# A fused four-layer network: 3x3 convolution in quarters with a fixed TensorE order, neighbour rankings in three steps, and quarter-size convolutions from contiguous copies

## The chip, the cores and the metric

One core of one Trainium2 chip runs the whole program as a single launch. The metric is the device time of that launch in microseconds. In a core, TensorE (PE in the profile; its weight loads are PEld) multiplies matrices from SBUF into PSUM, VectorE (DVE), ScalarE (ACT) and GpSimd (POOL) work on tiles in SBUF and PSUM, and DMA queues move data between the device's memory and SBUF; here nearly all bulk transfers are issued by SyncE (SP), and some by ScalarE. Each engine runs its own instructions in order and waits on semaphores for the others. Everything is float32.

## The reference, cut to what matters

`x` has shape (8, 64, 128, 128): eight images of 64 channels. Four layers follow each other, each with a residual and a group normalisation in front:

```python
x = x + deformable_conv(_gn(x), ...)    # layer 0
x = x + conv3x3(_gn(x), weight)         # layer 1: 64 -> 64 channels, padding 1
x = x + two_S5_blocks(_gn(x), ...)      # layer 2: one scan along rows, one along columns
x = x + neighbours(_gn(x), ...)         # layer 3
```

Layer 3, in short:

```python
x1 = relu(bnorm(conv2d(x, wd, bd, 4, 0)))          # 4x4 kernel, stride 4: 32x32 pixels remain
d2 = sq[:, :, None] + sq[:, None, :] - 2 * einsum("blc,bmc->blm", xt, xt)   # pixel to pixel
...                                                # window of 7x7 pixels, 9 largest distances
out = mean(x_final - xt[:, :, None, :], axis=2)    # mean of the nine picked, minus own
cat = concatenate([x1, out_img], axis=1)
feat = relu(bnorm(conv2d(cat, w1, b1, 1, 1)))      # 3x3, 128 -> 64 channels
att = sigmoid(bnorm(conv2d(mean(feat), wa)))       # one factor per image and channel
return resize(feat * att, 128x128, "bilinear")     # enlarged by 4
```

## The kernel before, in words

**Tiling.** Two images of 64 channels fill the 128 partitions, so there are four *pairs* of images. One pair is 128 x 16384 floats, and SBUF holds two such *rooms*. Layer 0 is done first for all pairs (most of its time is an indirect DMA that gathers pixels, L380, and VectorE's weighted sums of them, L391 and L392). It ends near 11700 us. Then `rest` (L496) takes the pairs p = 0 to 3 in turn: `conv3x3` (layer 1), `scan_layer` (layer 2), and `neighbours` (layer 3). The room that a pair doesn't fill holds that pair's normalised copy during the convolution; during the scans it is free, or receives the next pair.

**`neighbours` is a generator.** The one of pair p is not run when it is made; `conv3x3` of pair p + 1 is handed it as `aside`, and takes a step of it with `next(aside, None)` between its own operations. So three of the four convolutions (p = 1, 2, 3) have the previous pair's layer 3 beside them. Layer 3 of the last pair runs alone at the very end.

**`conv3x3` (L603 to L659).** Each of 16 loads normalises eight rows (L626, ScalarE) and SP's DMAs distribute them into `two`: row pairs on the free axis, and the odd and even rows of a pair on the two halves of the partitions, so that one product contracts 2 rows x 64 channels. The loop over n (16 steps) computes eight rows per image: for each parity e of the output row, each of two row pairs m, each of three column shifts dx and each image i there is a product (L647) of 128 x 64 weights with 4 rows of 128 pixels into the PSUM tile `c`, and the last is followed by an addition into the image (L651, VectorE). Where m is not e, half of the weights are zeros. For p = 0 these products are cut to *quarters*: only the half of the partitions whose weights are not zero, and products for e = 0 and e = 1 alternate, so that with the two images they use all four quarters of TensorE's array. For p = 1 to 3 the products are full: I call six products over all partitions a *block*; the quarters of a step, twelve products of a quarter of the array each, count as one too. A full step has four blocks, a step in quarters three (e = 0, the quarters, e = 1). Each float32 product has two records in the trace, so a full step has 48. There are three `next(aside)` per step. The program doesn't set the order between these products and those of `aside`; the Tile scheduler does, for every engine.

**`neighbours` (L1066 to L1181)** has three parts.

1. The quarter-size convolution, `quarter` (L983 to L1033) where a convolution is beside it: eight times, 16 rows of the stored image are loaded by four DMAs that ScalarE issues (L1007, three buffers), and 16 products (L1031) of 128 x 64 weights with 128 pixels read every fourth column of them, straight from the loaded rows; ScalarE's Relu (L1032) writes `x1`. For the last pair the image is still in SBUF, and `quarter_here` (L1035) reads it there: 16 taps x 2 images x 2 halves of the image, each product (L1055) with 512 pixels at a column step of four.
2. The ranking. For both images and each of eight pieces of 128 pixels, `farthest` (L1201) multiplies the piece with up to 320 pixels around it (L1207, the distance `d`), ScalarE adds the pixel's own square (L1211, `d2`), and VectorE does the rest: window (L1214, `key`), largest eight, replaced, the ninth, replaced, and a 0/1 `mask` (L1224). `means` (L1226) turns the mask with TensorE (L1232, `st`), ScalarE copies it (L1234, `sel`), and three products (L1238, `po`) with `xt` average the picked pixels into the second half of `cat` (L1239). `means` of a piece is called after `farthest` of the next. `features` (L1185) is the 3x3 convolution over `cat`, in four sets of 18 products (L1197, `pf`), and comes as soon as the pieces that it needs are done. Before the loop, `xt` (L1115) and the squares `own` (L1119) are made by TensorE, ScalarE and VectorE.
3. The enlarging. After the mean (L1137), the attention (L1142) and the scaled feature map (L1148, `wide`), each strip of eight small rows is widened (L1162 ScalarE, L1163 VectorE, into `up`), and for each of eight pieces of the image and each of four row phases VectorE adds two weighted rows of `up` onto the image (L1178, L1179: 64 operations of 128 x 512 in all), and SP stores the piece to `out` (L1180).

**The scans.** `scan_layer` runs class `Turns`: 16 groups of eight rows forward, then 16 more (`G >= NG`), all engines in an order written out by a planner. `at` (L1620) gives every operation a time, from the table `BESIDE` for the first half and `ALONE` for the second, plus a multiple of the group's planned length (26.969 and 27.485 us); the operations are sorted by that time and emitted under `manual_schedule()`. In the trace a group of the last scan's second half takes 13.19 us. Of one group, the operations used below are: `uv` (L1651, an addition on POOL), `xsb` and `xs` (L1662 and L1663, subtractions on POOL), `pn` (L1319) and the output products `py` (L1361) on TensorE, the turned copies `pt` (L1268, ScalarE), and the addition of a finished half group into the image, `add0` and `add1` (L1422, VectorE). For pairs 0 to 2 (`follow` is set) each finished group is also stored, `kept`, and the next pair is loaded beside; for the last pair neither happens.

Other rows that serve as prices: L1284 (ScalarE's normalisation in the scans, which reads every fourth element), L1282 and L1106 (POOL, a wide step and 1024 elements), L1531 (POOL, a copy of repeated elements).

Of the kernel before, what the change touches and what calls it, by code (L numbers as in the profile page):

```python
# [9 lines left out]
F32 = mybir.dt.float32  # L10
I32 = mybir.dt.int32
AF = mybir.ActivationFunctionType
ALU = mybir.AluOpType
# [3 lines left out]
P = 128  # L17
# [25 lines left out]
class Net:  # L43
# [452 lines left out]
    def rest(self):  # L496
        tc, nc = self.tc, self.nc
        with ExitStack() as ctx:
# [14 lines left out]
            for p in range(self.npair):  # L513
                now, other = rooms[p % 2], rooms[(p + 1) % 2]
                a, b = image(now), image(other)
                r, nb = self.conv3x3(p, a, other, *self.gn1, aside)
                norm = self.scan_layer(p, a, b, r, nb)
                aside = self.neighbours(p, None if p + 1 < self.npair else now[:, 0:HW], norm)
# [82 lines left out]

    def conv3x3(self, p, a, room, r, nb, aside):
# [8 lines left out]
        with self.tc.tile_pool(name=f"b_conv{p}", bufs=1) as cp, self.tc.tile_pool(name=f"b_conv2_{p}", bufs=2) as wp:  # L611
# [18 lines left out]
            for n in range(0, H // 2, 4):  # L630
                quarters = p == 0
                sets = []
                for e in range(2):
                    full = [(e, m, slice(0, P)) for m in range(2) if m == e or not quarters]
                    sets += [[(e, m, rows, dx) for dx in (0, -1, 1) for _, m, rows in full]]
                if quarters:
                    sets.insert(1, [(e, 1 - e, half[e], dx) for dx in (0, -1, 1) for e in range(2)])
                po = [None, None]
                left = [6, 6]
                for e, m, rows, dx in chain(*sets):  # L640
                    if po[e] is None:
                        po[e] = self.ps.tile([P, 4, H], F32, tag="b", name=f"c1_{p}_{n}_{e}")
                    c0, c1 = max(0, -dx), min(H, H - dx)
                    left[e] -= 1
                    for i in range(2):
                        mv = two[rows, i, n + m : n + m + 4, c0 + dx : c1 + dx]
                        nc.tensor.matmul(po[e][half[i], :, c0:c1], lhsT=w[rows, e, m, dx + 1], rhs=mv, start=left[e] == 5, stop=left[e] == 0)  # L647
                    if left[e]:
                        continue
                    rows = a[:, 2 * n : 2 * n + 8, :].rearrange("p (m e) w -> p e m w", e=2)[:, e]  # L650
                    nc.vector.tensor_add(rows, rows, po[e])  # L651
                    next(aside, None)
                for k in range(2):
                    g = n // 2 + k
                    nc.vector.bn_stats(st[:, g, :], a[:, 4 * g : 4 * g + 4, :].rearrange("p h w -> p (h w)"))
                next(aside, None)
            for _ in aside:
                pass
# [325 lines left out]
    def quarter(self, sp, p, src, norm, x1):  # L984
# [4 lines left out]
        with self.tc.tile_pool(name=f"b_down{p}", bufs=1) as wp, self.tc.tile_pool(name=f"b_down2_{p}", bufs=3) as yp:  # L989
# [13 lines left out]
            def load(n):  # L1003
# [4 lines left out]
                loaded.append(y.rearrange("p i (h m) (w g) -> p i h m w g", m=2, g=4))  # L1008
# [15 lines left out]
            for n in range(8):  # L1024
                if n + 2 < 8:
                    load(n + 2)
                yv = loaded.pop(0)
                pd = self.ps.tile([P, 4, S], F32, tag="x", name=f"pd{p}_{n}")
                for t in range(8):
                    for i in range(2):  # L1030
                        nc.tensor.matmul(pd[half[i]], lhsT=wr[i][:, t, :], rhs=yv[:, i, :, t // 4, :, t % 4], start=t == 0, stop=t == 7)  # L1031
                nc.scalar.activation(x1[:, n * P : (n + 1) * P], pd.rearrange("p h w -> p (h w)"), AF.Relu, bias=off, scale=self.bnd[0])  # L1032
                yield  # L1033

    def quarter_here(self, sp, p, af, norm, x1):  # L1035
# [4 lines left out]
        with self.tc.tile_pool(name=f"b_down{p}", bufs=1) as wp:  # L1040
# [8 lines left out]
            view = af.rearrange("p (h u f w g) -> p h f g u w", h=2, f=4, w=S, g=4)  # L1049
            pd = [self.ps.tile([P, L // 2], F32, tag="b", name=f"pd{p}_{i}") for i in range(2)]  # L1050
            for t in range(16):
                for i in range(2):
                    for h in range(2):
                        to = pd[i][half[h]].rearrange("p (u w) -> p u w", w=S)
# [11 lines left out]
    def neighbours(self, p, here, norm):  # L1066
# [3 lines left out]
        with tc.tile_pool(name=f"b_near{p}", bufs=1) as sp:  # L1070
# [10 lines left out]
            else:  # L1081
                yield from self.quarter_here(sp, p, here, norm, x1f)
            place = (lambda i, m: (m, i)) if here is None else (lambda i, m: (4 * i + m % 4, m // 4))
            with tc.tile_pool(name=f"b_far{p}", bufs=2) as wp:
# [8 lines left out]

                def filled(t, to, k):
# [17 lines left out]
                for m in range(2):  # L1112
                    tp = self.ps.tile([P, 4, P], F32, tag="y", name=f"xt{p}_{m}")
                    for k in range(4):
                        nc.tensor.transpose(tp[:, k, :], x1f[:, (4 * m + k) * P : (4 * m + k + 1) * P], self.ident)  # L1115
                    nc.vector.tensor_copy(xt[:, 4 * m : 4 * m + 4, :], tp)
                    sq = wp.tile([P, 8, C], F32, tag="sq", name=f"sq{p}_{m}", bufs=1)
                    nc.scalar.activation(sq.rearrange("p a c -> p (a c)"), tp.rearrange("p k c -> p (k c)"), AF.Square)
                    nc.vector.tensor_reduce(own[:, 4 * m : 4 * m + 4].rearrange("p k i -> p (k i)"), sq, axis=mybir.AxisListType.X, op=ALU.add)  # L1119
# [3 lines left out]
                late = None  # L1123
                for t in range(L // P):
                    for i in range(2):
                        mask = masks[0] if t == 0 else masks[3] if t == L // P - 1 else masks[1 + i]
                        self.farthest(wp, i, t, cat, xs, own, place, mask, f"{p}_{i}_{t}")
                        if late:
                            self.means(wp, *late)
                        late = i, t, mask, cat, xt, place, f"{p}_{i}_{t}"  # L1130
                        yield
                        if i == 0 and t in (3, 5, 7):
                            self.features(p, t // 2 - 1, cat, w1, feat, total, "x" if here is None else "b")
                self.means(wp, *late)
                self.features(p, 3, cat, w1, feat, total, "x" if here is None else "b")
# [7 lines left out]
            with tc.tile_pool(name=f"b_up{p}", bufs=2) as wp:  # L1143
# [8 lines left out]
                R = self.STRIP  # L1152
                for n in range(8):
                    if n % (R // 4) == 0:
                        h0 = 4 * n
                        up = wp.tile([P, R + 2, H], F32, tag="up", name=f"up{p}_{n}")
                        uv = up.rearrange("p h (w g) -> p h w g", g=4)
                        r0, r1 = max(0, h0 - 1), min(S, h0 + R + 1)
                        m0, m1 = r0 - h0 + 1, r1 - h0 + 1
                        for k, (side, w_side, w_mid) in enumerate(phases):  # L1160
                            t = wp.tile([P, R + 2, S], F32, tag="t", name=f"up_t{p}_{n}_{k}")
                            nc.scalar.mul(t[:, m0:m1], wide[:, r0:r1, 1 + side : S + 1 + side], w_side)  # L1162
                            nc.vector.scalar_tensor_tensor(uv[:, m0:m1, :, k], wide[:, r0:r1, 1 : S + 1], w_mid, t[:, m0:m1], ALU.mult, ALU.add)  # L1163
                        if h0 == 0:
                            nc.vector.tensor_copy(up[:, 0, :], up[:, 1, :])  # L1165
                        if h0 + R == S:
# [620 lines left out]
```

## Time and profile before

| | |
|---|---|
| runs | 15335.88, 15339.65, 15353.08 us; median 15339.65 |
| profiled execution | 15356.15 us, of which the span in the trace is 15354.2 |
| mean granted clock of TensorE | 0.821 |
| busy, share of the span | PE 66%, PEld 24%, DVE 75%, ACT 21%, POOL 68% |
| instructions | PE 32812, DVE 27082, ACT 5480, POOL 10624 |
| layer 0 and what it sets up | until some 11700 us |
| first convolution, first to last product | 11763.9 to 11893.6 us (130) |
| the three convolutions with layer 3 beside them | from 12523, 13419 and 14319 us: 271, 273, 271 |
| the last scan's second half | 14980 to 15195 us |
| the last pair's layer 3 | 15205 us to the end |

A row of a windows view has a stretch in us from the span's start, its length, and each engine's busy time in it with the number of instructions; then the clock that TensorE was granted (1.00 is full), the share of the DMA engines and the bytes moved. A row of a groups view has the line, the engine, the operation, what it writes <- what it reads with shapes, the number; after the bar the busy us, the mean ns of one, and the idle time before them with what ended it. A timeline row has the start, the duration, and the same names; brackets give a wait in us and who ended it.

### The profile page before, as it was taken

What the parts mean: (1) busy time and instruction counts of PE and PEld (TensorE: products, weight loads), DVE (VectorE), ACT (ScalarE), POOL (GpSimd) and SP (SyncE); (2) the same over time, 40 slices, a digit from 0 to 9 for tenths busy, and PEclk for the clock granted to TensorE, in tenths of its full rate; (3) what the DMA queues carried; (4) which work ended last, traced back from release to release, by engine and by line L of the source; (5) the groups of instructions that cost most, each with busy time, mean ns of one, the idle gap of its engine ahead of it and who ended that gap; (6) DMA issues with size and microseconds to landing.
All of it is one profiled execution on the core that took longest, in us unless ns stands there. A gap on an engine that the chain in (4) does not pass through costs nothing. (4 is left out here: it accounts for less than half of the span.)

```text
span 15354.2 us, 121942 instructions
## 1 busy us (share of the span) xinstructions
PE 10117.0 (66%) x32812; PEld 3654.0 (24%) x32812; DVE 11461.6 (75%) x27082; ACT 3228.7 (21%) x5480; POOL 10386.9 (68%) x10624
## 2 busy tenths in 40 slices
PE   7774477537765563577556656655434888899887
PEld 2211122112211111122111111111111444444443
DVE  6777777777777777777777777777775867858687
ACT  1100011001100000111000000000001855638374
POOL 5777777777777777777777777777773643617163
PEclk9986698759877786798777888887656999999998
DMA  5444454435543333444333333333333453544441
GB/s 175 125 123 132 122 152 154 125 116 153 154 130 113 115 116 111 138 150 127 114 114 115 116 115 115 118 117 110 108 108 121 107 138 115 141 113 125 130 105 54
DMA packets 888915, 1893.98 MB, mean 123 GB/s; under 512 B 198044, under 2 KB 447012, under 8 KB 866212
## 3 DMA queue, kind: packets, MB, share of 16 engines
q0 software_dynamic: 442368, 1208.55, 26.9%
q1 hardware_dynamic: 388192, 648.04, 14.0%
q10 hardware_dynamic: 57668, 29.59, 0.9%
q8 instruction: 265, 4.34, 0.1%
q14 instruction: 422, 3.46, 0.1%
HBM read 1524.22 MB, written 195.52 MB: 112 GB/s over the span
## 5 line engine op out<-in xcount | busy, mean ns | idle before, releaser
L380 POOL DMA_INDIRECT g<-table,idx x9216 | 8741.5, 949 | 2825.2 <-issue 2636.5
L391 DVE TENSOR_TENSOR g<-g,corner_weights 128x256 f32<-128x256 f32 x9216 | 3772.6, 416 | 2728.7 <-DMA g<-table,idx 2688.2
L392 DVE TENSOR_REDUCE sm<-g 128x64 f32<-128x256 f32 x9216 | 5014.0, 579 | 9.0
L292 PE MATMUL po<-xe,wt 128*54 128x512 f32 (+3 forms) x8384 | 4320.4, 631 | 13.2 <-ACT ob L302 12.4
L398 PE MATMUL sp<-ident,sm 128*128 128x128 f32 x4096 | 1538.6, 381 | 4159.9 <-DVE sm L392 4146.6
L403 ACT COPY s<-sp 128x512 f32<-128x512 f32 x1024 | 599.7, 586 | 8722.4 <-PE sp L398 8722.1
L398 PEld LDWEIGHTS sp<-ident,sm 128*128 128x128 f32 x4096 | 630.8, 156 | 6736.1 <-DVE sm L392 5022.2
L292 PEld LDWEIGHTS po<-xe,wt 128*54 128x54 f32 x8384 | 904.1, 132 | 1351.4 <-issue 1071.4
L409 PE MATMUL yp<-s,wd 128*64 128x512 f32 (+1 forms) x2560 | 899.6, 712 | 25.5 <-ACT s L403 24.8
L647 PE MATMUL c<-room,l_w 128*64 128x508 f32 (+2 forms) x3072 | 713.6, 606 | 49.5 <-DMA room<-nx 29.8
L1531 POOL COPY l_yb<-l_y 128x512 f32<-128x512 f32 x128 | 73.1, 616 | 825.2 <-DVE l_y L1526 825.2
L1284 ACT ACTIVATE fx<-room,ln_b,ln_g 128x512 f32<-128x512 f32 x472 | 596.2, 1313 | 25.1 <-DMA in<-fx 22.5
L1300 PE MATMUL pv<-in,tabs 128*128 128x512 f32 x1024 | 512.2, 633 | 81.8 <-DVE xt L1350 26.5
L1361 PE MATMUL py<-in,outs 128*128 128x512 f32 x1024 | 487.7, 599 | 0.0
L1361 PE MATMUL py<-x,outs 128*128 128x512 f32 x1024 | 481.8, 603 | 4.1 <-POOL x L1662 3.4
L1410 POOL TENSOR_TENSOR ms<-ms,y 128x512 f32<-128x512 f32 x256 | 265.6, 1049 | 311.5 <-DVE y L1405 252.9
L651 DVE TENSOR_TENSOR room<-room,c 128x512 f32<-128x512 f32 x128 | 87.0, 685 | 406.1 <-PE c L647 393.0
L402 PE MATMUL s<-ident,sm 128*64 128x128 f32 x512 | 176.9, 345 | 307.5 <-DVE sm L392 294.6
L400 PE MATMUL s<-ident,sm 128*64 128x128 f32 x1024 | 283.0, 368 | 125.7 <-DVE sm L392 123.6
L409 PEld LDWEIGHTS yp<-s,wd 128*64 128x64 f32 (+1 forms) x2560 | 260.7, 159 | 430.5 <-issue 314.6
L647 PEld LDWEIGHTS c<-room,l_w 128*64 128x64 f32 (+1 forms) x3072 | 250.4, 139 | 412.7 <-issue 347.1
L1378 PE MATMUL pc<-mix,h 64*128 64x128 f32 x4096 | 301.2, 286 | 54.9 <-POOL h L1673 30.2
(445 smaller groups left out, 9978.5 us busy)
## 6 DMA issues: line engine op xcount, KB each, us to landing
g<-table,idx POOLq DMA_INDIRECT x9216, 2.7
in<-fx SPq DMA_DIRECT2D x1008, 128.0 KB
xe<-in_x_dram SPq DMA_DIRECT2D x56, 1408.0 KB
table<-q SPq DMA_DIRECT2D x256, 256.0 KB
y<-ys SPq DMA_DIRECT2D x128, 256.0 KB
room<-in_x_dram SPq DMA_DIRECT2D x64, 512.0 KB
room<-nx SPq DMA_DIRECT2D x256, 128.0 KB
back<-z SPq DMA_DIRECT2D x120, 256.0 KB
```

The costliest lines, as they stand in the source:

```text
L292: nc.tensor.matmul(po[:, r0:r1, c0:c1], lhsT=wt[:, t, :], rhs=xe[:, row + r0 : row + r1, c0 + dx : c1 + dx], start=n == 0, stop=n == len(u ...
L380: nc.gpsimd.indirect_dma_start(out=tq[:, k, :], out_offset=None, in_=flat[i], in_offset=bass.IndirectOffsetOnAxis(ap=idx[:, at : at + 1], ...
L391: nc.vector.tensor_mul(t[:, ks], t[:, ks], w)
L392: nc.vector.tensor_reduce(sm[:, ks], t[:, ks].rearrange("p k q c -> p k c q"), axis=mybir.AxisListType.X, op=ALU.add)
L398: nc.tensor.transpose(sp[:, j, :], sm[:, j * P : (j + 1) * P], self.ident)
L403: nc.scalar.copy(st[i][:, :, m * P : (m + 1) * P], sp)
L409: nc.tensor.matmul(yp[half[i], :], lhsT=wd[rows, j, :], rhs=src[rows, :], start=j == 0, stop=j == 4)
L647: nc.tensor.matmul(po[e][half[i], :, c0:c1], lhsT=w[rows, e, m, dx + 1], rhs=mv, start=left[e] == 5, stop=left[e] == 0)
L1284: self.nc.scalar.activation(to, src, AF.Identity, bias=self.w["ln1_b"], scale=self.w["ln1_g"])
L1300: self.nc.tensor.matmul(pv, lhsT=self.tabs[:, at : at + P], rhs=fx[:, :, h, :], start=h == 0, stop=h == 1)
L1361: self.nc.tensor.matmul(py, lhsT=lt, rhs=mv, start=first and n == 0, stop=n == len(calls) - 1 and (fx is not None))
L1378: nc.tensor.matmul(pc[e][:, 2 * m + i], lhsT=hs[rows, i, m * P : (m + 1) * P], rhs=both, start=True, stop=True)
```

## The change

- **Convolutions.** All four use quarters. Their order is now fixed for TensorE alone (`manual_schedule(engines={PE})`); the other engines stay with the scheduler. Steps of `aside` are taken after given blocks: `due` says how many steps are to be done after block 0 to 47 (16 steps of three blocks). Ten steps (to the end of `quarter`) are spread over blocks 0 to 15, one comes at 16, twenty (the ranking) fall on blocks 18 to 22, and 13 (the enlarging) on the rest.
- **`quarter`.** Four ScalarE copies per load (two images x two row halves, 512 elements each, read at a column step of four) rearrange it into `yv`, one buffer, with each tap's 128 pixels contiguous; products read `yv`. Loads have two buffers instead of three.
- **`quarter_here`** reads a rearranged copy of the last image, `spread`, which the last scan makes in the free room: per group, two copies on POOL and two on ScalarE, 128 x 256 each, planned 8 us after `add1`.
- **Ranking.** `xt` and `own` come first. `means` is split: in each of 20 steps `farthest` of a piece comes with `turned` (transposes and `sel`) of the piece two before, and `means` of the piece three before. `features` come at steps 9, 13, 17 and 19.
- **Enlarging.** Each strip is widened one strip ahead. For the last pair alone, 11 of the 32 row phases go to TensorE: three products (two rows of `up` with scaled identities, and the image's row with the identity) add up in PSUM, and ScalarE copies the sum back.

```diff
+    def due(self, slot):
+        marks = [(0, 1), (3, 2), (15, 10), (16, 11), (17, 11), (22, 31), (47, 44)]
+        for (s0, n0), (s1, n1) in zip(marks, marks[1:]):
+            if slot <= s1:
+                return n0 + (n1 - n0) * max(0, slot - s0) // (s1 - s0)
+        return 99
...
-                quarters = p == 0
...
+            def beside(slot):
+                while done[0] < self.due(slot):
+                    done[0] += 1
+                    next(aside, None)
...
+            with self.tc.manual_schedule(engines={mybir.EngineType.PE}):
+                for k, n in enumerate(range(0, H // 2, 4)):
+                    po = [self.ps.tile([P, 4, H], F32, tag="b", name=f"c1_{p}_{n}_{e}") for e in range(2)]
+                    left = [6, 6]
+                    products(po, n, [(0, 0, every)], left)
+                    beside(3 * k)
+                    products(po, n, [(0, 1, half[0]), (1, 0, half[1])], left)
+                    add(po, n, 0)
+                    beside(3 * k + 1)
+                    products(po, n, [(1, 1, every)], left)
+                    add(po, n, 1)
+                    for g in (2 * k, 2 * k + 1):
+                        nc.vector.bn_stats(st[:, g, :], a[:, 4 * g : 4 * g + 4, :].rearrange("p h w -> p (h w)"))
+                    beside(3 * k + 2)
+                for _ in aside:
+                    pass
...
-    ... tc.tile_pool(name=f"b_down2_{p}", bufs=3) as yp:
+    ... tc.tile_pool(name=f"b_down2_{p}", bufs=2) as yp:
...
+                yv = wp.tile([P, 2, 2, 4, 4, S], F32, tag="yv", name=f"yv{p}_{n}")
+                for i in range(2):
+                    for m in range(2):
+                        nc.scalar.copy(yv[:, i, m], y[:, i, m])
...
-                        nc.tensor.matmul(pd[half[i]], lhsT=wr[i][:, t, :], rhs=yv[:, i, :, t // 4, :, t % 4], start=t == 0, stop=t == 7)
+                        nc.tensor.matmul(pd[half[i]], lhsT=wr[i][:, t, :], rhs=yv[:, i, t], start=t == 0, stop=t == 7)
...
-            view = af.rearrange("p (h u f w g) -> p h f g u w", h=2, f=4, w=S, g=4)
+            view = spread.rearrange("p (h n f g x) -> p h f g n x", h=2, f=4, g=4, x=2 * S)
...
+                for k in range(20):
+                    if k < 16:
+                        i, t, mask = pieces[k]
                         self.farthest(wp, i, t, cat, xs, own, place, mask, f"{p}_{i}_{t}")
+                    if 0 <= k - 2 < 16:
+                        i, t, mask = pieces[k - 2]
+                        picked[k - 2] = self.turned(wp, t, mask, f"{p}_{i}_{t}")
+                    if 0 <= k - 3 < 16:
+                        i, t, _ = pieces[k - 3]
+                        self.means(i, t, picked.pop(k - 3), cat, xt, place, f"{p}_{i}_{t}")
+                    if k in (9, 13, 17, 19):
+                        self.features(p, min(3, (k - 9) // 4 if k < 19 else 3), cat, w1, feat, total, ptag)
...
+                        if here is not None and (k == 3 or (k == 2 and n % 3 == 1)):
+                            ps = self.ps.tile([P, 4, H], F32, tag="xyb"[n % 3], name=f"sum{p}_{n}_{k}")
+                            for j, (lt, mv) in enumerate(((scaled[w_side], up[:, at + side : at + 4 + side, :]), (scaled[w_mid], up[:, at : at + 4, :]), (self.ident, rows))):
+                                nc.tensor.matmul(ps, lhsT=lt, rhs=mv, start=j == 0, stop=j == 2)
+                            nc.scalar.copy(rows, ps)
+                            continue
...
+    def spread(self, g):
+        src = self.a[:, 8 * g : 8 * g + 8, :].rearrange("p (u f) (w k) -> p f k u w", f=4, k=4)
+        to = self.b[:, 8 * g : 8 * g + 8, :].rearrange("p h w -> p (h w)").rearrange("p (f k u w) -> p f k u w", f=4, k=4, u=2)
+        for f in range(4):
+            (self.nc.gpsimd.tensor_copy if f % 2 else self.nc.scalar.copy)(to[:, f], src[:, f])
...
             if self.follow:
                 put("store", lambda: s.kept(g))
+            else:
+                self.at(G, "add1", lambda: s.spread(g), 8.0)
```

## The prediction

> **What bounds the kernel now.** I read the page's slices first, then the windows view of the stages that the change touches, then the groups, waits and timeline inside those. The deformable layer fills the first three quarters, and the order of its instructions is the same in both kernels, as is the first convolution's. So only four places count: the three convolutions that have a ranking beside them (starting 12523, 13419 and 14319 us; 271, 273 and 271 us), the second half of the last scan (14980 to 15195), and the last pair's ranking (15205 to the end). The windows view cuts the convolution at 12523 into loading and quarter size, ranking, and enlarging, and then gives the three late stretches:
>
> ```profile
> core 0: us, PE busy (x) PEld busy (x) DVE busy (x) ACT busy (x) POOL busy (x), PEclk, DMA share, GB/s
> 12523.00:12615.00 92.00, 84.95 (x489) 49.35 (x489) 14.06 (x34) 22.75 (x24) 0.00 (x0) 0.92 0.83 175
> 12615.00:12719.00 104.00, 103.96 (x564) 55.66 (x563) 57.05 (x172) 27.98 (x65) 2.99 (x5) 1.00 0.07 24
> 12719.00:12794.00 75.00, 66.42 (x298) 22.65 (x296) 65.59 (x112) 7.49 (x17) 0.00 (x0) 0.98 0.50 192
> 14980.00:15190.00 210.00, 195.23 (x963) 103.45 (x961) 187.95 (x385) 136.46 (x284) 129.27 (x105) 0.98 0.20 51
> 15205.00:15234.00 29.00, 28.89 (x131) 7.16 (x134) 0.47 (x3) 0.00 (x0) 0.00 (x0) 0.95 0.01 1
> 15299.00:15354.00 55.00, 0.00 (x0) 0.00 (x0) 49.51 (x85) 7.45 (x17) 0.00 (x0) 0.51 0.37 153
> ```
>
> TensorE sets the first two parts of a convolution, VectorE nearly all of the third (its ends overlap, so 65.6 of 75 busy is no slack: the operations follow each other every 0.60 us). ScalarE has 69 us free in the first part. The last scan half is tight on TensorE and VectorE; the last stretch is VectorE alone. Three groups carry prices (page and groups view; after the bar: busy us, mean ns of one):
>
> ```profile
> L1284 ACT ACTIVATE fx<-room,ln_b,ln_g 128x512 f32<-128x512 f32 x472 | 596.2, 1313 | 25.1 <-DMA in<-fx 22.5
> ```
> ```profile
> L626 ACT ACTIVATE nx<-room,gn_nb,gn_y 128x1024 f32<-128x1024 f32 x16 | 19.7, 1240 | 67.2 <-DMA room<-nx 43.3 <-DMA yq<-y 20.7 <-DMA norms<-norm 3.2
> L1031 PE MATMUL pd<-yq,l_wr 128*64 128x128 f32 x256 | 35.6, 407 | 0.0
> ```
>
> L626 reads whole rows: 1024 elements in 1.24 us, 0.62 per 512. L1284 reads every fourth element of a row (or whole columns): 512 in 1.31. The new copies read every fourth element.
>
> **Convolutions, gain.** Before, pairs 1 to 3 send full products: 24 records take 5.0 us in the timeline, 10.2 us for the 48 of one step. The first convolution already uses quarters: 768 records from 11763.9 to 11893.6, 8.1 us a step, 2.70 for each of its three blocks. That is at most 16 x 2.1 = 34 us of TensorE per convolution. What is late next, part by part:
>
> First part. The fixed order puts the last of the eight quarter-size products (L1031's) after 16 of 48 blocks: 16 x 2.7 = 43 us of convolution, against some 48 before. But each needs four new ScalarE copies of 512 elements at a step of four, 1.31 each by L1284, into a single buffer; the loads (now two buffers) are issued on the same engine behind them. The first copies can start after the fifth normalisation, 17.5 us in. Behind that ScalarE has 11 x 1.24 + 32 x 1.31 + 8 x 0.45 + 24 issues x 0.61 = 74 us in one stream, and some 10 us of waits where a copy needs the buffer that the product before it still reads: 102 us, not 92. The products themselves go from 3.7 us to between 1.9 and 3.7, which ScalarE hides. **+10.** If copies cost 0.62 the part is some 87 us, set by TensorE and the loads.
>
> Ranking part. Twenty steps now sit in five blocks. VectorE's order (read from the built kernels) is mostly one ranking after the other: alone, one took 3.22 us (key at 12653.25, mask done 12656.47). Twelve at 3.22 are 39, two interleaved pairs of short ones 4.5 each, additions of the convolution 3, the fill in front (two blocks, transposes, first distance) 10, and behind the last mask the turn, the mean and two feature sets (19.3 / 4 = 4.8 each) 12, mean and attention 3: 76 us against 104. TensorE's own sum, 51 of ranking and 5 x 2.7, is 65, under it. **-28.**
>
> Enlarging part. VectorE: 64 x 0.60 + 16 x 0.61 + 35 x 0.61 for nine steps of the convolution + 2 = 72 us, and TensorE 25 blocks, 68 us. They hold each other: a block needs the PSUM tile that the addition two before it frees, and those additions stand behind runs of enlarging. Followed row by row, the last two steps of the convolution come after the last enlarging operation, 9 us: 81 against 75. **+6.** Sum per convolution 259 against 271: -12, three times **-36**.
>
> **Last scan, loss.** Rearranging the last image adds, per group of eight rows, two copies of 256 elements on POOL and two on ScalarE. The plan's times do not hold: a group takes 13.19 us, not 27.5. POOL's, TensorE's, VectorE's and ScalarE's rows of one group:
>
> ```profile
> 15035.58 1.28 POOL L1663 TENSOR_TENSOR x<-x,xt 128x512 f32<-128x512 f32 x1 [1.29 <-DVE xt L1350]
> 15036.81 1.28 POOL L1662 TENSOR_TENSOR x<-x,xt 128x512 f32<-128x512 f32 x1
> 15039.49 1.28 POOL L1651 TENSOR_TENSOR uu<-uu,uv 128x512 f32<-128x512 f32 x1 [1.40 <-DVE uv L1313]
> ```
> ```profile
> 15037.68 0.38 PE L1319 MATMUL pn<-z,tabs 128*128 128x2 f32 x2 [0.30 <-DVE room L1422]
> 15038.14 1.98 PE L1361 MATMUL py<-x,outs 128*128 128x512 f32 x4
> ```
> ```profile
> 15036.55 1.07 DVE L1422 TENSOR_TENSOR room<-room,tp 128x512 f32<-128x512 f32 x1
> ```
> ```profile
> 15036.38 1.15 ACT L1268 COPY pt<-pv 64x512 f32<-64x512 f32 x2 [0.76 <-PE pv L1300]
> ```
>
> L1361 starts as L1662 ends (15038.09): no slack. In the changed order the POOL copies stand between L1663 and L1662 and wait for the addition L1422, done at 15037.62. One is unknown; bounds are 0.30 (L1531, 616 ns for 512 repeated elements) and 0.96 (L1282, 1918 ns for 512 at a wide step); I take 0.65, the middle, for the step is wide but the work is a plain copy. Then L1662 ends at 37.65 + 1.3 + 1.28 = 40.2 and TensorE is 2.1 us late. It comes back: this addition ends 12.67 us after the L1361 of its turn began, so the turn is 12.67 + 1.3 + 1.3 = 15.3 us. ScalarE's copies (0.66 each), in front of L1268, make a loop of 15.2. Fourteen groups have copies there: 14 x 2.1 = **+30** (bounds 22 to 39).
>
> **Last ranking, gain.** The 32 quadrant products of the quarter-size convolution follow each other every 0.90 us at a step of four; the first convolution's quadrants, equally long but contiguous, every 0.43. 32 x 0.45 = 14.4 instead of 28.8: -14. Starting own and xt earlier and taking means three steps late saves 1 us in front and 3 behind the last mask (12.7 us from it to the last features; st, po and one feature set are 9.5): -4. Of 64 enlarging operations 22 leave VectorE: 22 x 0.60 = 13; in their place TensorE does 33 products of 0.85 (28 us) and ScalarE 11 copies, both beside VectorE's 36; the last two rows wait for them 1 us: -12. Cover gone would cost those 28 us. Together **-30**.
>
> **Sum.** -36 + 30 - 30 = -36 us. The profiled execution took 15356.15 (span 15354.2), 16.5 above the median of the runs, 15339.65. I move the median: **15304**.
>
> [...]
>
> **Rivals.** *Copies are cheap* (0.2): ScalarE takes 0.62, the first part falls to 87 us, each convolution gains 27; POOL and ScalarE at their low ends cost 22. -81 + 22 - 30 = -89: 15251. For it: no row shows exactly this copy. Against: L1284.
> *It cancels* (0.25): the enlarging part's mutual waits take 8 us more per convolution and POOL's copies are at 0.96: -12 + 39 - 30 = -3: 15337. For it: TensorE can no longer fill a wait with other work.
> *The fixed order stalls* (0.13, slower): in the ranking, TensorE stands before a mask with the next distance queued behind it, so VectorE gets it late. Beyond 12 / 16 = 0.75 us per ranking a convolution loses; at 1.4 us more (4.6 instead of 3.22) it is 22 us each: 15304 + 66 = 15370. For it: 15 us of waits for distances (L1211's ACT) even with a free order. Against: two distances are always out ahead.
> That the change does not do what it says: the built order shows quarters and fixed places, so I give it no share of its own.
>
> **Numbers.** Forecast 0.42, its own spread 15285 to 15325. Range 15250 to 15365, which leaves out the far half of the slower case and what lies under the cheap one. 0.2% is 31 us, about what a measurement tells from no change: faster is the cheap case, and some 0.27 of the forecast's 0.42: 0.47; slower nearly the stalling case: 0.13; the same 0.40.
>
> **What would show it.** Right: yv copies near 1.3 us and TensorE idle before the quarter products; rankings about 75 us; groups of the last scan near 15.3 us with POOL waiting for L1422; the last quarter products 14 us; no VectorE gap after 15300. Wrong: groups still at 13.2 us, yv copies near 0.6, or TensorE waiting more than 20 us for masks.

## The result, and the profile after

The changed kernel is **slower**: 15471.4 us (15465.5 to 15496.5, four runs) against 15339.27 (15335.88 to 15353.08, four runs); the ratio is 1.0088, 95% interval 1.0077 to 1.0100. I had forecast 15304 and a range that ended at 15365. The profiled execution took 15496.5 us (span 15494.7), 140 more than that of before.

Both traces can be cut at the same events. "First part" is from the first normalisation (`nx`) of a convolution to the first `key`, "ranking" from there to `wide`, "enlarging" from `wide` to the convolution's last product (mean of three convolutions, us):

| | first part | ranking | enlarging | convolution, first to last product | last scan, to the first quarter-size product | tail |
|---|---|---|---|---|---|---|
| before | 100.5 | 96.1 | 70.5 | 262.7 | 618.7 | 149.1 |
| after | 106.7 | 120.7 | 83.8 | 306.7 | 652.5 | 124.6 |
| change | +6.2 | +24.6 | +13.3 | +44.0 | +33.8 | -24.5 |
| predicted | +10 | -28 | +6 | -12 | +30 | -30 |

Three convolutions, the last scan and the tail are 132 + 34 - 24.5 = 141 us; the stretches between the convolutions give 6 back. The windows view of the same stages as in the prediction (the last scan's row is again 210 us out of its second half):

```profile
core 0: us, PE busy (x) PEld busy (x) DVE busy (x) ACT busy (x) POOL busy (x), PEclk, DMA share, GB/s
12529.00:12635.00 106.00, 80.10 (x574) 39.81 (x574) 22.29 (x42) 61.86 (x64) 2.99 (x5) 0.88 0.74 155
12635.00:12755.00 120.00, 74.44 (x380) 43.28 (x382) 46.60 (x151) 22.73 (x56) 0.00 (x0) 0.73 0.05 18
12755.00:12843.00 88.00, 73.55 (x396) 21.47 (x392) 72.48 (x122) 7.25 (x17) 0.00 (x0) 0.97 0.46 174
15140.00:15350.00 210.00, 177.75 (x816) 93.17 (x815) 156.86 (x325) 130.61 (x267) 126.33 (x115) 0.93 0.18 43
15370.00:15387.00 17.00, 16.20 (x136) 6.07 (x136) 0.79 (x4) 0.42 (x1) 0.00 (x0) 0.87 0.01 2
15453.00:15495.00 42.00, 30.53 (x66) 12.89 (x66) 35.68 (x63) 13.09 (x27) 0.00 (x0) 0.87 0.49 200
```

In the ranking TensorE fell from 104 busy of 104 to 74 of 120, and VectorE is idle too: 47 of 120. No engine is the bound there; they wait for each other in a circle. The waits view of that part (after the colon: total us, times, longest) names both ends of it:

```profile
engine line waited for: us in total, times, longest us
ACT sel L1283 <- PE st L1281: 50.4, 13, 4.7
DVE key L1263 <- ACT d L1260: 50.1, 12, 8.2
PE st L1281 <- DVE mask L1273: 44.5, 11, 4.6
```

VectorE's `key` waits for a distance, TensorE's `st` waits for a mask. In the ranking of before the first wait was small, and TensorE had the distance `d` ahead of the transposes `st`:

```profile
DVE key L1214 <- ACT d L1211: 11.5, 5, 4.9
```

```profile
12651.85 0.81 PE L1207 MATMUL d<-xs,cat 128*128 128x320 f32 x2
12652.49 0.49 PE L1232 MATMUL st<-ident,mask 128*128 128x128 f32 x3
```

One turn of the changed kernel, on VectorE, TensorE and ScalarE (timeline rows):

```profile
12656.77 0.33 DVE L1273 TENSOR_SCALAR mask<-key 128x320 f32<-128x320 f32 x1
12661.56 0.49 DVE L1263 SCALAR_TENSOR_TENSOR key<-d,window 128x320 f32<-128x320 f32 x1 [4.46 <-ACT d L1260]
...
12664.52 0.33 DVE L1273 TENSOR_SCALAR mask<-key 128x320 f32<-128x320 f32 x1
12669.24 0.49 DVE L1263 SCALAR_TENSOR_TENSOR key<-d,window 128x320 f32<-128x320 f32 x1 [4.39 <-ACT d L1260]
```

```profile
12657.25 0.87 PE L1281 MATMUL st<-ident,mask 128*128 128x128 f32 x3 [3.96 <-DVE mask L1273]
12658.05 1.54 PE L1293 MATMUL po<-sel,xt 128*64 128x128 f32 x6
12659.52 1.44 PE L1256 MATMUL d<-xs,cat 128*128 128x320 f32 x2
12664.90 0.90 PE L1281 MATMUL st<-ident,mask 128*128 128x128 f32 x3 [3.94 <-DVE mask L1273]
```

```profile
12661.00 0.53 ACT L1260 ACTIVATE d<-d,own 128x320 f32<-128x320 f32 x1 [1.09 <-PE d L1256]
```

Here `st` starts 0.15 us after the *newest* mask is done, and the distance `d` of the next piece stands behind it on TensorE. But `st` belongs to the piece two before, whose mask was done long ago. The code says why: in a step `farthest` of piece k comes first, and it writes `masks[1 + i]`; `turned` of piece k - 2 then reads `masks[1 + i]`, the same buffer. So in program order the transposes read what piece k wrote, and must wait for it. For ten of the 16 pieces the changed kernel thus averages with the mask that was written for the piece two later; its time is to be read with that in mind. (The kernel before has a small case of the same: the two images share `masks[0]` for their first pieces and `masks[3]` for their last, and the mask of the second image is written before that of the first is turned. This holds for two of 16 pieces, in the kernel before and in every run below.) With TensorE's order fixed, every such wait holds back the next distance: mask, `st`, `po`, `d`, ScalarE, `key`, mask, 7.65 us a piece.

### The profile page after: what moved, and what is told of

The parts are those of the page before. It is cut to its first block, busy times and chain, and to the rows that moved or that the text cites. A ratio compares the mean times of both kernels' runs of the same rounds, so it can differ in the third digit from the quotient of the medians.

```text
span 15494.7 us, 122229 instructions
## 1 busy us (share of the span) xinstructions
PE 10050.7 (65%) x32878; PEld 3608.5 (23%) x32878; DVE 11452.0 (74%) x27060; ACT 3355.1 (22%) x5619; POOL 10409.7 (67%) x10660
## 5 line engine op out<-in xcount | busy, mean ns | idle before, releaser
L654 PE MATMUL c<-room,l_w 128*64 128x508 f32 (+3 forms) x3072 | 574.6, 624 | 59.2 <-DVE room L658 29.7
L1416 PE MATMUL py<-x,outs 128*128 128x512 f32 x1024 | 491.2, 613 | 32.1 <-POOL x L1724 32.1
L1416 PE MATMUL py<-in,outs 128*128 128x512 f32 x1024 | 489.8, 601 | 0.0
L1433 PE MATMUL pc<-mix,h 64*128 64x128 f32 x4096 | 301.0, 286 | 54.9 <-POOL h L1735 30.5
L1477 DVE TENSOR_TENSOR room<-room,tp 128x512 f32<-128x512 f32 x256 | 297.5, 1162 | 32.6 <-PE tp L1472 31.6
```

What stands on the lines that cost most here:

```text
L1416: self.nc.tensor.matmul(py, lhsT=lt, rhs=mv, start=first and n == 0, stop=n == len(calls) - 1 and (fx is not None))
L1433: nc.tensor.matmul(pc[e][:, 2 * m + i], lhsT=hs[rows, i, m * P : (m + 1) * P], rhs=both, start=True, stop=True)
```

## The experiments

Some chips ran layer 0 in 14.8 ms instead of 11.8, the kernel before as well (18400 us in all). The stages after layer 0 took the same on all chips (first convolution 130.0 to 131.1 us everywhere), so besides ratios to runs on the same chip I compare stage lengths, and the time from the second convolution's first product to the end (2826.4 us before, 2961.6 after). Ratios are to the kernel before, with 95% intervals. The end of layer 0 also differs between kernels on one chip: the first convolution starts at 11738 and 11735 us in f1_quarters and f3_shared, at 11767 and 11765 us in f2_joined and f5_direct. Totals of single runs therefore say little here, and stages decide.

### More mask buffers (e1_masks)

```diff
-  masks = [... for k in range(4)]
+  masks = [... for k in range(6)]
-  masks[0] if t == 0 else masks[3] if t == L // P - 1 else masks[1 + i]
+  masks[0] if t == 0 else masks[5] if t == L // P - 1 else masks[1 + (2 * t + i) % 4]
-  new = lambda name: wp.tile(..., tag=name, ...)[:, 0:n]
+  new = lambda name: wp.tile(..., tag=name, ..., bufs=2 if name == "d2" else 1)[:, 0:n]
```

> The changed kernel with a ring of four mask buffers for the inner pieces, so that the ranking of a piece no longer writes the buffer from which the piece two before is still to be turned (room for it: key and left have one buffer each). The turned mask is thus that of the piece it is used for, where the changed kernel turns the one written two pieces later. Theory A (the shared mask buffer): the 44 us that each of the last three convolutions lost come mostly from a circle: TensorE's transposes wait for the mask that was just begun, and the next distance is queued behind them (7.65 us a piece). Then the ranking's first to last key falls from 106.6 us to some 60, each convolution from 306 us to 255-265, and the whole from 15471 to some 15330-15345. Theory B (the fixed order by itself: TensorE stands before any mask with distances behind it): the ranking stays above 95 us and the whole above 15440.

Measured: first to last key 54.6 us (106.9 after), ranking 68.3, convolutions 252.4; to the end 2811.6; ratio 0.9990 (0.9975 to 1.0005). Theory A, with shorter convolutions than its 255 to 265 us. The ranking is now 27.8 us shorter than before the change, where I had predicted 28. The last pair's ranking takes 72.7 us here instead of 66.6; that it comes from `key` and `left` having one buffer each was not tried.

### The same buffers, turned first (e2_turned_first)

```diff
+  picked[k - 2] = self.turned(...)    # if 0 <= k - 2 < 16
   self.farthest(...)                  # piece k
-  picked[k - 2] = self.turned(...)
```

> The changed kernel with one pair of statements swapped: in each step the mask of the piece two before is turned ahead of the distance of the new piece; four mask buffers as in the changed kernel. The turned mask is that of its own piece again. Theory A: the transposes now wait for a mask finished a piece ago, one distance is always out: ranking 60-65 us, whole 15330-15350, near the run with more buffers. Theory B: TensorE waits for a mask in every step with the distance directly behind it; the ranking stays above 95 us, the whole above 15440.

Measured: first to last key 54.8 us, ranking 68.6, convolutions 253.3; to the end 2805.2; ratio 0.9991 (0.9979 to 1.0004). Theory A again, though the ranking lies above its 60 to 65 us. Without a byte more memory the circle is gone; its waits are, for the same part of the convolution (waits view):

```profile
ACT sel L1283 <- PE st L1281: 26.2, 13, 5.7
...
PE st L1281 <- DVE mask L1273: 11.6, 6, 5.5
...
DVE key L1263 <- ACT d L1260: 10.9, 10, 2.5
```

VectorE waits 10.9 us for distances instead of 50.1. The longest wait for a mask that is left, 5.5 us, ends with the second image's first mask, which lies in the buffer that the first image's first piece reads.

### The shared buffers in a free order (e3_free)

```diff
-  with self.tc.manual_schedule(engines={mybir.EngineType.PE}):
+  if True:
```

> The changed kernel without the fixed order for TensorE in the convolutions: the scheduler orders TensorE as it does the others; shared mask buffers stay. Theory A: the circle needs both the shared buffer and the fixed order; a free order can put the next distances ahead of the waiting transposes, so the ranking comes down to 75-85 us and the convolutions to 265-280 us: whole 15360-15410. Theory B: the fixed order alone is at fault, so the convolution falls below what it was before, 245-260 us, whole 15320-15345.

Measured: first to last key 48.5 us, ranking 70.1, enlarging 76.0 (83.8 after), convolutions 246.6; to the end 2790.1; ratio 0.9976 (0.9962 to 0.9990). My numbers for theory A were too high, and rival B's 245 to 260 us for the convolution is right for this run. The two runs above refute B as the sole cause all the same. What stands is an **interaction**: the ranking takes 120.7 us with both the shared buffers and the fixed order, 68.3 and 68.6 with the fixed order alone, 70.1 with the shared buffers alone, and 67.8 with neither (f2_joined below). The 52 us need both. The fixed order has a smaller price of its own, 6 us a convolution, most of it in the enlarging.

### The copies of the last image, 3.3 us later (e4_spread_late)

```diff
-  self.at(G, "add1", lambda: s.spread(g), 8.0)
+  self.at(G, "add1", lambda: s.spread(g), 11.3)
```

> The changed kernel with the copies of the last image planned 11.3 us after add1 instead of 8.0: on GpSimd they then stand behind the subtraction L1724 that releases TensorE's output products instead of ahead of it. Theory A: the 34 us that the last scan lost come from that subtraction standing behind copies that wait for the addition into the image; a group falls from some 15.3 us to 13.2-13.8, and the whole from 15471 to 15440-15450. Rival: the copies cost by their amount, on GpSimd and ScalarE, wherever they stand: no more than 5 us gained.

Measured: last scan 616.9 us against 652.5, groups 13.34 us apart (the mean of 14 in the changed kernel is 15.85); to the end 2928.6, 33 less than after; ratio 1.0059 (1.0039 to 1.0078), with the circle still in. The rows of GpSimd and TensorE in one group, first of the changed kernel:

```profile
15190.95 1.21 POOL L1488 COPY room<-room 128x256 f32<-128x256 f32 x2 [0.83 <-DVE room L1477]
15192.11 1.28 POOL L1724 TENSOR_TENSOR x<-x,xt 128x512 f32<-128x512 f32 x1
```

```profile
15193.45 3.67 PE L1416 MATMUL py<-x,outs 128*128 128x512 f32 x4 [2.12 <-POOL x L1724]
```

and then of this run:

```profile
18232.75 1.28 POOL L1724 TENSOR_TENSOR x<-x,xt 128x512 f32<-128x512 f32 x1
18233.97 1.24 POOL L1488 COPY room<-room 128x256 f32<-128x256 f32 x2
```

```profile
18234.08 1.98 PE L1416 MATMUL py<-x,outs 128*128 128x512 f32 x4
```

Same copies, same durations, behind the subtraction instead of ahead of it, and TensorE no longer waits. The place was the price, not the amount.

### Quarters alone (f1_quarters)

```diff
-  quarters = p == 0
+  quarters = True
```

> The kernel before with quarters in all four convolutions and nothing else changed; the scheduler orders TensorE. The convolution of pairs 1 to 3, from first to last product, took 263 us before, 306 in the changed kernel and 247 in the changed kernel with a free order. Theory A: the quarters are what gains (34 us of TensorE taken out, of which ScalarE's and VectorE's stretches give back a half): 243-252 us. Rival: the gain of the run with the free order is that of the three-step ranking; quarters alone give 256-263 us, because the ranking and the enlarging are bound by other engines.

Measured: convolutions **268.3** us, slower than the full products' 262.7; ranking 102.3 against 96.1, the other parts as before; to the end 2861.7, 35 more than before (17 in the convolutions, 18 in the scans between them, whose cause I did not look for). Both theories missed, A by 16 us. (The whole took 15367.62 us, one run, against 15367.03 on this chip: what the stages lose is hidden by layer 0, which ended some 29 us earlier than in f2_joined.) Two things in the trace say why. First, three steps of `aside` still go with each step of the convolution, so the ranking holds 245 records of the convolution where it held 228: less work per product moves nothing into the parts that have room. Second, the scheduler takes the quarter products apart. From one record's start to the next, within uninterrupted runs, a quarter record takes 0.113 us in the first convolution, 0.127 in the fixed order of the changed kernel, 0.150 in the free order of e3_free and 0.159 here (full ones 0.225 to 0.253). Short waits are in these means: here the 24 blocks that stay whole have 0.147, the broken ones 0.173. Three runs of quarter records between other work in this kernel's timeline, of four, six and two records, take the same time:

```profile
12622.49 1.07 PE L647 MATMUL c<-room,l_w 64*64 64x508 f32 x4
...
12624.29 1.08 PE L647 MATMUL c<-room,l_w 64*64 64x508 f32 x6
...
12630.16 1.06 PE L647 MATMUL c<-room,l_w 64*64 64x508 f32 x2
```

So in the ranking the quarters keep TensorE busy for 64.2 us, where the full products took 63.0.

### Three mends together (f2_joined)

The edits of e2_turned_first, e3_free and e4_spread_late.

> The changed kernel with three mends together: TensorE's order free, the mask of the piece two before turned ahead of the new piece's distance, the copies of the last image planned 11.3 us after add1. If the costs are separate they add: convolutions 244-250 us against 263 before, last scan 617 (from the end of the last convolution to the first product of the last quarter-size convolution) as before, the end 122-125 against 149; so 70-80 us below the kernel before. Rival: with the turned masks ahead, a free order gains nothing over the fixed one in the ranking, convolutions 252, some 60 us below.

Measured: convolutions 247.0, last scan 619.9, tail 120.6; to the end 2748.8, 78 less than before; 15288.13 us against 15367.03 on the same chip, ratio 0.9950 (0.9933 to 0.9966). The costs add; the rival falls.

### Half of the new copies on GpSimd (f3_shared)

```diff
-  nc.scalar.copy(yv[:, i, m], y[:, i, m])
+  (nc.gpsimd.tensor_copy if m else nc.scalar.copy)(yv[:, i, m], y[:, i, m])
```

> The joined version, with half of the new copies of the quarter-size convolution (those of the second row half) on GpSimd, which does nothing else there. Theory A: ScalarE's stream of copies (32 of 1.12 us) is what holds the first part at 104-106 us from the first normalisation to the first key; with 16 copies fewer it falls to 93-98 us. Rival: the loads of the image and the normalised rows (their DMAs) set it: it stays above 102 us.

Measured: first part 104.5 us (106.0 in f2_joined), to the end 2743.9. The rival: ScalarE is busy 44 us of the first part instead of 61, and the part is 1.5 us shorter, so ScalarE's sum doesn't set it.

### No copies (f5_direct)

```diff
-  yv = wp.tile(...); nc.scalar.copy(...) x4;  rhs=yv[:, i, t]
+  rhs=y[:, i, :, t // 4, :, t % 4]            # bufs=3
```

> The joined version without the new copies: the quarter-size products read the loaded rows at a column step of four, as before the change, with three buffers. Products then take 3.7 us a set by the row of the kernel before instead of 2.2. Theory A: ScalarE's copies hold the first part; without them it falls from 104 to 92-98 us and the convolution to 236-243 us. Rival: TensorE, which gives back 8 x 1.6 = 13 us, becomes the bound: the first part stays above 102 us.

Measured: first part 100.9, ranking 65.7, convolutions 241.7; to the end 2728.8, 20 less than f2_joined; one run of 15263.22. The convolution is where A put it, the first part is not: 5 us less, and back at the 100.5 of before. The copies buy TensorE time (the 256 records of the quarter-size convolution keep it busy 22.9 us in the changed kernel, 35.6 before) that it doesn't need there.

### Half of the quarter-size loads (g1_halfload)

```diff
-  load(1)
...
-  if n + 2 < 8: load(n + 2)
-  y = loaded.pop(0)
+  if n % 2 == 0 and n + 2 < 8: load(n + 2)
+  y = loaded[n // 2]
```

> The version without the new copies, with every second load of the quarter-size convolution left out (its products use the rows of the load before again, so half of that convolution's rows are not those of the reference); this takes 4.2 MB of the 16.8 MB out of the first part of each convolution. Theory A: the transfers (16.8 MB in 100 us) hold the first part at 98-106 us, whatever ScalarE and TensorE do; it falls to 78-88 us. Rival: the latency of the normalised rows (two buffers, ScalarE waiting 20 to 40 us for them) or the order of the steps holds it: it stays above 95 us.

Measured: first part 91.3, between both theories; to the end 2704.2. A quarter fewer bytes give a tenth less time, so the loads hold part of the first part; whether by their bytes or by their issuing on ScalarE, which the edit halves too, and what holds the rest, stays open.

### Six PSUM tiles for the convolution's second half (g2_psum)

```diff
-  tag="b"
+  tag="b" if k < 8 else "byx"[k % 3]
```

> The version without the new copies (free order), with the convolution's PSUM tiles of the second half of its steps taken from three tags in turn instead of one, so six tiles instead of two. Theory A: in the enlarging, TensorE and VectorE hold each other through two tiles, and the convolution's last products come 8 to 15 us after the last enlarging operation; with six tiles the enlarging falls from 79 to 71-75 us, VectorE's own sum, and the whole by 12-24 us below 15263. Rival: VectorE's order, set by the scheduler, holds the additions back however many tiles there are: 78-80 us.

Measured: the last enlarging operation ends 66 to 68 us after `wide`, and the convolution's last product after 62 (79.5 in f5_direct). Ratio 0.9928 (0.9911 to 0.9944), **with that of the next run the lowest that has an interval**; to the end 2719.4, 9 less than f5_direct. The windows and the waits of the enlarging, f5_direct first:

```profile
12695.00:12778.00 83.00, 69.84 (x376) 20.04 (x375) 71.07 (x121) 7.22 (x16) 0.00 (x0) 0.97 0.47 185
```

```profile
PEld c L654 <- DVE room L658: 16.8, 9, 3.1
PE c L654 <- DVE room L658: 9.3, 7, 2.2
DVE room L658 <- PE c L654: 8.9, 4, 3.3
```

and g2_psum:

```profile
15764.00:15830.00 66.00, 61.90 (x374) 18.77 (x372) 62.56 (x107) 7.21 (x16) 0.00 (x0) 0.99 0.54 207
```

```profile
PEld c L654 <- DVE room L658: 0.3, 1, 0.3
```

The mutual waits are gone and VectorE is busy 62.6 of 66. Of the 49 us that the three convolutions gained, 40 are lost again in the stretches behind them (644.3, 647.8 and 630.6 us instead of 631.6, 635.5 and 616.0). Most of that is the mark: with six tiles TensorE's products run ahead, and VectorE's additions and statistics come after the last of them. TensorE's next instruction waits for those statistics (`gn_mv`), f5_direct first and then g2_psum:

```profile
PE gn_pm L129 <- DVE gn_mv L146: 3.2, 1, 3.2
```

```profile
PE gn_pm L129 <- DVE gn_mv L146: 12.0, 1, 12.0
```

They end 3.1 us behind the last product in f5_direct and 11.9 to 13.8 here. From `wide` to their end the part falls from 82.6 to 74.9 us, and a convolution from 244.8 to 238.3: 20 us for the three, of which the scans lose 10 again. Theory A's 71 to 75 us, VectorE's own sum, is where VectorE ends, though by the last product, for which it was stated, the part took 62; its 12 to 24 us for the whole were not reached. Why the scans lose 10 was not tried.

### The same in the fixed order (g4_fixed_psum)

The edit of g2_psum, with the changed kernel's `manual_schedule` for TensorE kept.

> As the run with six tiles, but with TensorE's fixed order of the changed kernel (and the mask turned ahead, no new copies, the later copies of the last image). In a fixed order the quarter products stay together (0.127 us a record, against 0.149 in the free order). Theory A: with the circle and the two-tile lock gone, the fixed order is as good as the free one: convolutions 236-243 us, total within 15 us of the free run. Rival: the fixed order's waits (for masks, for the quarter-size rows) remain, convolutions 246-252 us, 20-40 us slower.

Measured: convolutions 231.1 us, to the end 2734.4, ratio 0.9926 (0.9908 to 0.9943). Theory A, and below its range for the convolutions (to the end of the statistics 240.6 us, against 238.3 in the free order): 15 us behind the free order by stages, and not to be told from it in the runs. Quarter records take 0.111 us here, as in the first convolution.

## Why the prediction was wrong, step by step

- **Ranking, predicted -28, measured +24.6: the step that failed.** I wrote "Twelve at 3.22 are 39" and, against the stalling rival, "two distances are always out ahead". I had followed the order of the instructions, not whose buffer the waiting one reads. What failed is the overlap: a wait of the transposes for the newest mask, which I put at nothing, stops the next distance, and each turn takes 7.65 us. The sign that I had named for being wrong, TensorE waiting more than 20 us for masks, came: 44.5. With that one dependency mended the ranking comes out at -27.8 (e1_masks) and -27.5 (e2_turned_first). The missed term is 52 us a convolution, 157 in all; the forecast plus 157 is 15461, measured 15471. The other misses have both signs, and that they come to only 10 us is luck: in the two mended runs the stages to the end are 15 and 21 us below those of before, where I had forecast 36.
- The rival *the fixed order stalls* had the right mechanism, "TensorE stands before a mask with the next distance queued behind it", though not its reason, the shared buffer, and a price of 1.4 us a ranking where a turn of the circle costs 7.65 - 3.29 = 4.4 (3.29 is one ranking alone, from `key` at 12661.56 to the end of `mask` at 12664.85).
- **First part, predicted +10, measured +6.2.** The copies took 1.13 us, not 1.31 (groups view of this part):

```profile
L1049 ACT COPY yv<-yq 128x512 f32<-128x512 f32 x32 | 34.1, 1130 | 0.0
```

  The direction held, the reason only in part. ScalarE's single stream of 102 us is not what sets it (f3_shared), and "if copies cost 0.62 the part is some 87 us" is not borne out by f5_direct, which has none (its products read at a step of four again) and takes 100.9; no run has copies at that price.
- **Enlarging, predicted +6, measured +13.3.** The mechanism was right, each side waiting for the other through two PSUM tiles (g2_psum, and in the fixed order g4_fixed_psum, where this part takes 65.8 us); the convolution's end behind the last enlarging operation, which I put at 9 us, was 14 to 19 in the changed kernel.
- **What bounds a part.** "TensorE sets the first two parts" was wrong for the first: in f1_quarters TensorE is busy 87 us there instead of 93, and the part stays as it was. For the ranking of before no run contradicts it, for the quarters taken apart kept TensorE busy 101.5 us of 102.3. But the busy share didn't tell how much TensorE got done there: two quarter records showed as 1.06 us of work and six as 1.08.
- **Last scan, predicted +30, measured +33.8.** Right in mechanism and terms: a wait of 2.12 us before L1416 (2.1 predicted), 0.64 us a copy (0.65). The group became 15.85 us instead of 15.3; the four records behind the wait took 3.67 us instead of 1.98, which I had not counted, and how much of the half microsecond comes from that was not tried. The copies' rows (source view):

```profile
L1488 ACT COPY room<-room x32: 636/654/680, 15127.7 to 15361.1; 128x256 f32<-128x256 f32 x32
L1488 POOL COPY room<-room x32: 624/640/660, 15128.0 to 15362.2; 128x256 f32<-128x256 f32 x32
```
- **Tail, predicted -30, measured -24.5.** Products 16.1 us instead of 29.1 (-13, predicted -14; the rounds of four records, side by side on the quarters of the array, follow each other every 0.43 us as assumed, as single records over the whole array do in L1224, but the first five rounds took 0.85), enlarging 41.9 instead of 54.9 (-13, predicted -12, with TensorE's sums beside it as assumed), ranking +1.5 instead of -4; with the mask turned first (f2_joined) it is -2.4. In the groups of the last stretch VectorE's 42 operations and TensorE's 33 products stand side by side:

```profile
L1224 PE MATMUL sum<-up,scaled 128*128 128x512 f32 x44 | 22.4, 634 | 5.7 <-issue 5.0 <-DVE up L1199 0.6
L1227 DVE SCALAR_TENSOR_TENSOR room<-up,room 128x512 f32<-128x512 f32 x21 | 13.8, 695 | 0.0
L1228 DVE SCALAR_TENSOR_TENSOR room<-up,room 128x512 f32<-128x512 f32 x21 | 13.8, 693 | 0.0
```

- **The step of four** cost time, as I had taken from L1284 and from the rounds of before: a ScalarE copy of 512 elements at that step took 1.13 us, where L626 takes 0.62 for as many contiguous ones (1.24 for 1024), and a round of four contiguous records of the last image took 16.1 / 32 = 0.50 us against 0.90.

## What to carry to other kernels

The transposes, moved later past the instruction that writes their buffer, waited for the newer write (11 times, 44.5 us in a ranking): before trusting "one is always out ahead", name the buffer that the waiting instruction reads, and who writes it next in program order. In the fixed order such a wait also held everything behind it on TensorE, so the same mistake cost some 2 us in a free order (70.1 against 67.8) and 52 us in the fixed one (120.7 against 68.3 and 68.6). Taking work off an engine gained here only where the part that it held received less of it: quarters alone lost, quarters with a new distribution gained.

## What the runs showed of the hardware that was not expected

- In the stalled ranking the granted clock of TensorE was 0.73, where the busy ranking of before had 1.00, and the stalled instructions themselves took longer: three transposes 0.87 to 0.90 us instead of 0.49, a distance 1.44 instead of 0.81 (from 12657 to 12661 us, in which they ran, the granted clock was 0.51). That lengthens each turn of the circle by more than a microsecond.
- Quarter products gained only in company: 0.113 us a record in the unbroken blocks of the first convolution, 0.173 in the blocks of f1_quarters that the scheduler broke up, where two records alone took as long as six; a full record took 0.225 to 0.253.
- At a step of four the clock made no difference. The contiguous rounds of the last image took 0.85 us at a granted clock of 0.50 (15370 to 15374.5 us) and 0.43 at 1.00; the rounds of before, at a step of four, took 0.90 at 0.65 (15205 to 15209 us) as at 1.00.
